# Three transposes of a four-layer kernel: from the tensor engine to 32x32 blocks on the vector engine and DMAs through DRAM

## The chip, the cores and the metric

The kernel runs on one core of a Trainium2 chip. The metric is the device time of one execution in microseconds, the lower the better. One launch computes all 32 batches; all data are float32.

## What is computed

Four residual layers follow one another on `x` of 32 batches x 256 tokens x 256 features:

```python
# L0: attention of 16 heads of 16, queries and the own key from fside
q = (seq2 + b_self) @ Wq + bq
k = concat([seq1 + b_prev, seq2 + b_self], 1) @ Wk + bk
v = concat([seq1, seq2], 1) @ Wv + bv
score_prev = q . k[:, :, :l1] * SCALE        # masked by seq_len1
score_self = (q * k[:, :, l1:]).sum(-1) * SCALE
weights = softmax(concat([score_prev, score_self], -1))
attn = weights[..., :-1] @ v[:, :, :l1] + weights[..., -1:] * v[:, :, l1:]
x = x + (attn @ Wo + bo)                                   # x1
# L1: adapter of 64, its weights chosen by a batch's id
a = x + relu(x @ W1[id] + b1[id]) @ W2[id] + b2[id]
x = x + (layernorm(a) * gamma[id] + beta[id])              # x2
# L2: linear layer chosen by a batch's id
x = x + (x @ weight[id].T + bias[id])                      # x3
# L3: pooling
scores = tanh(x @ W1 + b1) @ v
p = softmax(where(mask[type], scores[:, None, :], -1e30), -1)
x = x + (p @ x) / count(mask)
```

## The kernel before

Batches are handled in 16 pairs (`p`), two batches `i` to a pair, `b = 2 * p + i`. Each step of the work is a small function (`proj_q`, `s1`, `row_max`, ...), and tables place every call: ONCE for the set-up, FIRST, SECOND, SLOTS, NEXT_TO_LAST and LAST for the pairs 0, 1, 2 to 13, 14 and 15. A place plus 16 (`PERIOD`) for each pair is sorted, and the calls are made in that order. So the order in which each engine gets its instructions is written out by hand; the places are no times, only an order. A pair's table spans some 75 places, so four or five pairs are in the work at once: while pair `p` is in its attention, pair `p - 1` is in the adapter and pair `p - 2` in the pooling.

The attention of a batch has eight score steps, in one PSUM tile `s` of 128 x 2048 that exists once. Four of them are `s1` (L1404): the scores, which `row_max` (L1421) reads on the vector engine to find the largest of each row. The other four are `s2` (L1512): the scores again with the keys on the partitions and the maxima taken off inside the product; `exps` (L1530) reads them on the scalar engine. The maxima get into the product by DMAs on SyncE's queue: `max_own` (L1444) writes them into rows of `q`, `ones_rows` (L1433) ones into rows of `k`, `own_exp` (L1459) the own weights into `epad`. `av` multiplies by the values, `av_blocks`, `sums` and `with_own` finish the division, `att_T` (L1579) transposes by 32x32 blocks on the vector engine (the heads are laid out so that blocks are enough), and `out_proj` and `x1_out` end the first layer.

Three times after that a matrix of 256 x 256 of each batch is needed with its features (or keys) on the partitions, and each time it is transposed by the tensor engine: `x1_T`, `x2_T` and `pr_T` call `transposed` (L1157), four products with the identity into one PSUM tile; `x1T_out`, `x2T_out` and `prT_out` call `from_psum` (L1169), a copy by the scalar engine into a tile of tag `T`, which has four buffers and is shared with `attT`. The readers are `hidden` (x1), `pool_hidden` and `subject` (x2) and `pooled` (the pooling weights, which stand in `mb`).

All small products go through three PSUM tiles of tag `g`. SyncE's queue issues nearly all DMAs, in the order of the tables: `load_T` (the transposed inputs), `load_x`, `load_adapter`, `load_subject`, `load_pool`, the small ones of the attention, and `store`. `q_out` (L1325) scales the queries on the vector engine. `setup_warm` (L1047) multiplies zeros of `epad` while the first loads are under way.

Of the kernel before, what the change touches and what calls it, by code (L numbers as in the profile page):

```python
# [9 lines left out]
F32 = mybir.dt.float32  # L10
# [6 lines left out]
P = 128  # L17
# [19 lines left out]
    (("setup_warm", 2), -106.0922),  # L37
    (("setup_load", "wq"), -75.9765),
    (("setup_load", "lang"), -72.4551),
    (("setup_load", "wk"), -70.4394),  # L40
    (("setup_warm", 0), -67.4191),
    (("setup_len",), -53.0448),
    (("setup_q",), -51.9044),
    (("setup_load", "subj"), -49.8615),
    (("setup_ones",), -44.2931),
    (("setup_load", "ptype"), -33.949),
    (("setup_heads",), -33.6815),
    (("setup_warm", 1), -25.0685),
    (("setup_load", "wo"), -23.0732),
    (("setup_ks",), -19.1134),  # L50
    (("setup_load", "bo"), -16.1547),
    (("setup_k",), -14.712),
    (("setup_tw_load", 0), -14.4792),
    (("setup_mcol",), -14.1846),
    (("setup_load", "wv"), -11.1214),
    (("setup_xconst",), -6.1757),
    (("setup_tw_load", 1), -3.8083),
    (("setup_load", "pw"), -1.98),
    (("setup_vbc",), -1.4711),
    (("setup_tw_bias",), 2.7996),  # L60
    (("setup_tw", 0), 6.7491),
    (("setup_tw", 1), 7.9258),
    (("setup_tw_load", 3), 8.1898),
    (("setup_tw_load", 2), 10.5556),
    (("setup_tw", 2), 12.4314),
    (("setup_tw_load", 5), 12.6441),
    (("setup_tw", 3), 16.9719),
    (("setup_tw_load", 4), 18.7648),
    (("setup_tw", 4), 21.2344),
    (("setup_tw_load", 7), 22.4248),  # L70
    (("setup_tw", 5), 23.4443),
    (("setup_tw_load", 6), 27.4787),
    (("setup_pool",), 29.3991),
    (("setup_tw", 6), 30.1493),
    (("setup_tw", 7), 35.4648),
# [4 lines left out]
    (("load_T", "fT"), -18.0603),  # L80
    (("load_T", "xT"), -16.5929),
    (("key_mask", 0), -15.9223),
    (("mask_keys", 0), -11.5916),
    (("key_mask", 1), -9.8727),
    (("proj_q", 0), -4.2691),
    (("q_out", 0), -4.1714),
    (("mask_keys", 1), -2.9814),
    (("self_values", 0), -2.5097),
    (("vs_blocks", 0), -1.9691),
    (("proj_k", 0), -1.7792),  # L90
    (("k_out", 0, 1), -1.0305),
    (("k_out", 0, 0), -0.6291),
    (("proj_k", 1), 1.188),
    (("s1", 0, 0), 1.2724),
    (("row_max", 0, 0), 1.4111),
    (("proj_q", 1), 1.5198),
    (("k_out", 1, 0), 1.8917),
    (("k_out", 1, 1), 1.9044),
    (("q_out", 1), 2.5716),
    (("load_x",), 2.935),  # L100
    (("s1", 0, 1), 3.5652),
    (("spread_q", 0, 1), 3.7902),
    (("row_max", 0, 1), 4.0616),
    (("proj_ks", 0), 4.2676),
    (("spread_q", 1, 0), 4.4707),
    (("proj_v", 0), 4.7177),
    (("spread_q", 0, 0), 5.6696),
    (("s1", 0, 2), 5.7766),
    (("ks_out", 0), 5.7846),
    (("row_max", 0, 2), 6.3321),  # L110
    (("v_out", 0), 6.8578),
    (("proj_v", 1), 6.9271),
    (("s1", 0, 3), 7.4456),
    (("proj_ks", 1), 7.7548),
    (("row_max", 0, 3), 7.8712),
    (("v_out", 1), 7.9003),
    (("ones_rows", 0), 8.4374),
    (("s1", 1, 0), 9.1884),
    (("ks_out", 1), 9.471),
    (("row_max", 1, 0), 9.6756),  # L120
    (("own",), 9.894),
    (("own_out",), 10.0239),
    (("max_T", 0), 10.7096),
    (("spread_q", 1, 1), 10.865),
    (("s1", 1, 1), 11.0673),
    (("max_own", 0), 11.4623),
    (("row_max", 1, 1), 11.7033),
    (("s2", 0, 0), 11.7624),
    (("exps", 0, 0), 11.8784),
    (("own_exp", 0), 12.3792),  # L130
    (("s1", 1, 2), 13.3753),
    (("row_max", 1, 2), 13.7856),
    (("x_bias",), 13.9304),
    (("s2", 0, 1), 14.101),
    (("exps", 0, 1), 14.6396),
    (("s1", 1, 3), 15.0742),
    (("av", 0, 1), 15.3164),
    (("av", 0, 0), 15.4106),
    (("row_max", 1, 3), 15.4873),
    (("max_T", 1), 15.7138),  # L140
    (("s2", 0, 2), 15.8427),
    (("max_own", 1), 16.0723),
    (("exps", 0, 2), 16.1397),
    (("own_blocks", 0), 16.1874),
    (("av_blocks", 0, 0), 16.4114),
    (("s2", 0, 3), 18.02),
    (("sums", 0, 0), 18.0472),
    (("weighted", 0), 18.0754),
    (("exps", 0, 3), 18.7005),
    (("av", 0, 2), 18.9332),  # L150
    (("ones_rows", 1), 18.9624),
    (("s2", 1, 0), 20.3742),
    (("own_exp", 1), 20.473),
    (("exps", 1, 0), 21.6941),
    (("av", 0, 3), 22.9145),
    (("s2", 1, 1), 22.9621),
    (("self_values", 1), 23.0582),
    (("exps", 1, 1), 23.1594),
    (("with_own", 0, 0), 23.1667),
    (("av_blocks", 0, 1), 23.5299),  # L160
    (("vs_blocks", 1), 23.5391),
    (("sums", 0, 1), 23.8644),
    (("av", 1, 0), 23.9519),
    (("with_own", 0, 1), 24.0779),
    (("att_T", 0), 24.0955),
    (("s2", 1, 2), 24.7815),
    (("own_blocks", 1), 24.7831),
    (("out_proj", 0), 24.8791),
    (("exps", 1, 2), 25.1475),
    (("x1_out", 0), 25.405),  # L170
    (("load_adapter", 1), 25.9774),
    (("av", 1, 1), 26.02),
    (("av_blocks", 1, 0), 26.1355),
    (("s2", 1, 3), 26.4333),
    (("sums", 1, 0), 26.723),
    (("load_adapter", 0), 26.729),
    (("weighted", 1), 26.7904),
    (("exps", 1, 3), 26.8359),
    (("with_own", 1, 0), 27.1301),
    (("av", 1, 3), 27.2786),  # L180
    (("av", 1, 2), 27.3089),
    (("av_blocks", 1, 1), 28.4885),
    (("sums", 1, 1), 29.1552),
    (("x1_T", 0), 29.1691),
    (("x1T_out", 0), 29.2343),
    (("with_own", 1, 1), 29.2714),
    (("att_T", 1), 29.5256),
    (("out_proj", 1), 29.7422),
    (("x1_out", 1), 30.3052),
    (("load_subject",), 30.8005),  # L190
    (("x1_T", 1), 32.0886),
    (("x1T_out", 1), 33.0458),
    (("hidden",), 34.2518),
    (("x1_beta", 0), 34.292),
    (("x1_beta", 1), 34.8076),
    (("x1_b2", 1), 35.1038),
    (("x1_b2", 0), 35.2963),
    (("h_out",), 35.6535),
    (("adapted",), 35.9027),
    (("y_out", 0), 36.1405),  # L200
    (("y_out", 1), 36.5261),
    (("norm_stats", 0), 37.0676),
    (("norm_stats", 1), 37.0951),
    (("norm_rstd", 0), 37.6476),
    (("norm_shift", 0), 37.6554),
    (("norm_rstd", 1), 38.2154),
    (("load_pool",), 38.2983),
    (("norm", 0), 38.4629),
    (("x2_out", 0), 39.0849),
    (("x2_T", 0), 39.3257),  # L210
    (("x2T_out", 0), 39.4394),
    (("norm_shift", 1), 39.8435),
# [1714 lines left out]
```

## Time and profile before

| | us |
|---|---|
| median of 3 runs | 1056.31 |
| the three runs | 1054.40, 1056.43, 1056.31 |
| the profiled execution, its own time | 1057.54 |
| its span in the profile | 1055.7 |

| engine | busy us | share of the span | instructions |
|---|---|---|---|
| PE (TensorE) | 1035.9 | 98% | 7940 |
| DVE (VectorE) | 738.6 | 70% | 1239 |
| ACT (ScalarE) | 515.5 | 49% | 722 |
| POOL (GpSimd) | 361.9 | 34% | 489 |

The DMA engines moved 81.08 MB in 58985 packets; the packets of SyncE's queue took 25.2% of the time of 16 engines.

How to read the lines: a row of a group gives the source line, engine, operation, output <- input with their shapes and the count; then busy time and the mean duration of one in ns; then the idle time of the engine just before these instructions, and what ended it. A row of the timeline gives the start in us, the time, engine, line and operation, with the number of instructions merged into it; times of neighbouring matmuls overlap, so differences of starts are used for what one costs. The waits rows name who waited for whom: us in total, times, longest. SPq is SyncE's queue.

### The profile page before, as it was taken

Reading aid. Unit: us, or ns where it says so; the run is one execution under the profiler, and the core shown is the slowest. Engines: PE = TensorE matmul, PEld = TensorE weight load, DVE = VectorE, ACT = ScalarE, POOL = GpSimd, SP = SyncE. Lnnn points to the kernel's source line nnn. Section 1 sums busy time; section 2 is a strip of 40 time slices with the busy share of each in tenths; the row PEclk is TensorE's granted clock in tenths of the full one; section 3 lists DMA queues with packets and bytes.
Section 4 is the critical chain, followed back from the end, with each engine's and each line's share of the span. In section 5 each row is a group of like instructions: output and inputs, shape, how many; then the busy total and the mean of one; then the engine's idle time right before and its main releaser. Section 6 shows DMA issues by size and latency. Waiting matters only on the chain.

```text
span 1055.7 us, 20836 instructions
## 1 busy us (share of the span) xinstructions
PE 1035.9 (98%) x7940; PEld 599.9 (57%) x7940; DVE 738.6 (70%) x1239; ACT 515.5 (49%) x722; POOL 361.9 (34%) x489
## 2 busy tenths in 40 slices
PE   8999999999999999999999999999999999999997
PEld 5555555555555555555555556556555565555656
DVE  3766676776767677676767768677676767767675
ACT  1243454536455455554554454554545545454553
POOL 3022544233343243243324233333324323324262
PEclk9999999999999999999999999999999999999999
DMA  6131321232232211323132132312322222121231
GB/s 207 32 90 61 92 62 44 76 98 83 62 98 70 89 59 47 108 72 97 46 94 72 52 107 73 87 53 79 91 92 61 78 78 82 43 59 61 69 95 51
DMA packets 58985, 81.08 MB, mean 77 GB/s; under 512 B 7238, under 2 KB 40774, under 8 KB 58886
## 3 DMA queue, kind: packets, MB, share of 16 engines
q1 hardware_dynamic: 58358, 78.18, 25.2%
q8 instruction: 63, 1.03, 0.4%
q10 hardware_dynamic: 288, 0.79, 0.2%
q0 software_dynamic: 240, 0.79, 0.2%
q14 instruction: 36, 0.29, 0.1%
HBM read 68.45 MB, written 9.71 MB: 74 GB/s over the span
## 4 chain that ended last, share of the span: by engine, by line
PE 92%; DVE 3%; ACT 3%; DMA 1%; issue 1%; POOL 0%; SPq 0%; DVEq 0%; ACTq 0%; POOLq 0%
PE s L1521 13%; PE s L1412 13%; PE av L1543 11%; PE ksps L1313 6%; PE v_ps L1180 5%; PE qps L1313 5%; PE o_ps L1180 5%; PE p_ps L1180 5%; PE vs_ps L1180 5%; PE kps L1313 5%; PE z_ps L1180 5%; ACT e L1533 2%; PE y_ps L1654 2%; PE h_ps L1628 2%; PE t_ps L1737 2%; PE x1T_ps L1162 2%
## 5 line engine op out<-in xcount | busy, mean ns | idle before, releaser
L1533 ACT ACTIVATE e<-s 128x2048 f32<-128x2048 f32 x128 | 240.3, 1877 | 396.0 <-PE s L1521 396.0
L1425 DVE TENSOR_REDUCE nmpad<-s 128x8 f32<-128x2048 f32 x128 | 293.2, 2290 | 173.1 <-PE s L1412 172.7
L1521 PE MATMUL s<-q,k 32*128 32x256 f32 x2048 | 146.7, 400 | 3.1 <-DVE nmpad L1425 2.4
L1412 PE MATMUL s<-k,qc 32*128 32x512 f32 x1024 | 146.0, 640 | 2.5 <-ACT e L1533 1.0
L1543 PE MATMUL av<-e,vpad 128*32 128x256 f32 x2048 | 130.6, 383 | 0.0
L1521 PEld LDWEIGHTS s<-q,k 32*128 32x128 f32 x2048 | 92.5, 184 | 59.8 <-issue 25.9
L1574 POOL TENSOR_TENSOR vs<-bt,vs 128x256 f32<-128x256 f32 x64 | 46.9, 733 | 213.5 <-DVE bt L1555 213.5
L1543 PEld LDWEIGHTS av<-e,vpad 128*32 128x32 f32 x2048 | 57.6, 109 | 80.5 <-issue 39.6
L1412 PEld LDWEIGHTS s<-k,qc 32*128 32x128 f32 x1024 | 40.0, 183 | 46.5 <-ACT e L1533 29.7
L1313 PE MATMUL qps<-fT,wqs 128*128 128x512 f32 x128 | 65.1, 632 | 0.0
L1180 PE MATMUL o_ps<-wos,attT 128*128 128x256 f32 x256 | 62.7, 388 | 2.4 <-DVE pnmx L1775 1.8
L1180 PE MATMUL vs_ps<-fT,wvs 128*128 128x256 f32 x256 | 63.7, 392 | 0.0
L1180 PE MATMUL v_ps<-wvs,xT 128*128 128x256 f32 x256 | 63.5, 391 | 0.1
L1313 PE MATMUL ksps<-fT,wks 128*128 128x512 f32 x128 | 63.3, 617 | 0.0
L1313 PE MATMUL kps<-xT,wks 128*128 128x512 f32 x128 | 63.2, 617 | 0.0
L1180 PE MATMUL z_ps<-ws,x2T 128*128 128x256 f32 x256 | 62.4, 387 | 0.0
L1340 ACT ACTIVATE k<-kps,kbias,cols 128x512 f32<-128x512 f32 x64 | 46.9, 782 | 30.7 <-PE kps L1313 30.5
L1180 PE MATMUL p_ps<-x2b,prT 128*128 128x256 f32 x256 | 60.8, 381 | 0.0
L1575 POOL TENSOR_TENSOR vs<-vs,zs 128x256 f32<-128x256 f32 x64 | 39.7, 620 | 58.3 <-DVE zs L1565 56.1
L1180 PEld LDWEIGHTS vs_ps<-fT,wvs 128*128 128x128 f32 x256 | 46.1, 189 | 20.9 <-issue 12.6
L1680 POOL TENSOR_SCALAR rstd<-mv 128x2 f32<-128x2 f32 x32 | 7.9, 248 | 142.3 <-DVE mv L1673 142.3
L1180 PEld LDWEIGHTS o_ps<-wos,attT 128*128 128x128 f32 x256 | 46.8, 190 | 16.8 <-issue 5.9
(134 smaller groups left out, 1522.4 us busy)
## 6 DMA issues: line engine op xcount, KB each, us to landing
an<-in_adn SPq DMA_DIRECT2D x32, 384.0 KB
mk<-pool_d SPq DMA_DIRECT2D x32, 257.0 KB
fT<-in_fT SPq DMA_DIRECT2D x16, 512.0 KB
xs<-in_x SPq DMA_DIRECT2D x32, 256.0 KB
ws<-in_swT SPq DMA_DIRECT2D x32, 256.0 KB
out<-x2b SPq DMA_DIRECT2D x32, 256.0 KB
xT<-in_xT SPq DMA_DIRECT2D x15, 512.0 KB
wb<-in_sb SPq DMA_DIRECT2D x32, 128.0 KB
```

The costliest lines, as they stand in the source:

```text
L1162: nc.tensor.transpose(ps[:, cc, q * P : (q + 1) * P], src[:, q, cc * P : (cc + 1) * P], ident,)
L1180: nc.tensor.matmul(ps[:, q, :n], lhsT=lhsT(c, q), rhs=rhs[:, c, :], start=(c == 0), stop=(c == 1),)
L1313: nc.tensor.matmul(ps, lhsT=w[:, ci, c * P : (c + 1) * P], rhs=T[src, p][:, ci].rearrange("p b s -> p (b s)"), start=(ci == 0), stop=(ci = ...
L1340: nc.scalar.activation(joint("k", p, work, [P, 2, 2, 2, S])[:, u, c].rearrange("p b s -> p (b s)"), T["kps", p, c], AF.Identity, bias=kbia ...
L1412: nc.tensor.matmul(ps[:, j], lhsT=T["qc", p][r, c, i, q * P : (q + 1) * P], rhs=T["k", p][r, :, c, i, :], start=True, stop=True,)
L1425: nc.vector.tensor_reduce(nm_bufs[i][:, q, g : g + 8].rearrange("p (u j) -> p j u", u=2), T.pop(("s1", b, n)), AX.X, ALU.max, negate=True,)
L1521: nc.tensor.matmul(ps[:, j, k, :], lhsT=T["k", p][r, u, c, i, k * P : (k + 1) * P], rhs=T["q", p][r, u, c, i, :], start=True, stop=True,)
L1533: nc.scalar.activation(e, T.pop(("s2", b, n)), AF.Exp)
L1543: nc.tensor.matmul(ps[j * HB : (j + 1) * HB, u, :], lhsT=v_bufs[b % 3][:, k, 8 * c + 2 * j + u, :], rhs=e[:, j, k, :], start=(k == 0), sto ...
L1574: nc.gpsimd.tensor_tensor(vs, bt[:, :, :, 0:DH], vs, ALU.add)
L1575: nc.gpsimd.tensor_tensor(vs, vs, z.unsqueeze(3).to_broadcast([P, S // HB, 2, DH]), ALU.mult)
L1628: nc.tensor.matmul(ps[i * A : (i + 1) * A, :], lhsT=T["a1", b][:, c * A : (c + 1) * A], rhs=T["x1T", b][:, c, :], start=(c == 0), stop=(c ...
```

## The change

For the pairs 0 to 13 the three transposes go another way. `blocks` transposes 32x32 blocks on the vector engine (one instruction for 128 x 512), `to_dram` stores them with four DMAs, one for each group of 32 partitions, in pieces of 32 floats, so that the blocks stand in `swap_d` in the order of the transposed matrix, and `from_dram` loads it back with one DMA of 2 KB for each partition. `from_dram` waits for the stores of its matrix. The block tiles have a tag `bl` with two buffers, shared with the set-up's `sw`. NEXT_TO_LAST and LAST, the pairs 14 and 15, keep `x1_T`, `x1T_out` and the like. The transposed tiles are laid out with the row half ahead of the column half in both ways, and their readers index them so. Besides, `q_out` moves from the vector to the scalar engine; `setup_warm` reads a tile `fill` of ones, which is set first, and is called six times, not three; and every place in all six tables is new.

```diff
+    fill = work.tile([P, S], F32, tag="th", name="fill", bufs=1)
+    nc.gpsimd.memset(fill, 1.0)
...
     def setup_warm(n):
...
         for _ in range(2):
-            nc.tensor.matmul(ps, lhsT=epad[:, 0:P], rhs=epad, start=True, stop=True)
+            nc.tensor.matmul(ps, lhsT=fill[:, 0:P], rhs=fill, start=True, stop=True)
...
     def transposed(b, src, name):
-        ps = g_tile(f"{name}_ps{b}").rearrange("p (c s) -> p c s", c=2)
-        for cc in range(2):
-            for q in range(2):
-                nc.tensor.transpose(
-                    ps[:, cc, q * P : (q + 1) * P],
-                    src[:, q, cc * P : (cc + 1) * P],
-                    ident,
-                )
+        ps = g_tile(f"{name}_ps{b}").rearrange("p (q c s) -> p q c s", q=2, c=2)
+        for q in range(2):
+            for c in range(2):
+                nc.tensor.transpose(ps[:, q, c, :], src[:, q, c * P : (c + 1) * P], ident)
         T[f"{name}_ps", b] = ps
...
+    NAMES = ("x1", "x2", "pr")
+
+    def blocks(p, i, name):
+        b = 2 * p + i
+        src = T["mb" if name == "pr" else name, b]
+        bl = work.tile([P, 4, 4, HB], F32, tag="bl", name=f"{name}bl{b}", bufs=2)
+        nc.vector.transpose(
+            bl.rearrange("p k n r -> p (k n r)"),
+            src.rearrange("p q (c k e) -> p k (q c) e", c=2, e=HB),
+        )
+        T[name, "bl", b] = bl
+
+    def to_dram(p, i, name):
+        b = 2 * p + i
+        bl = T.pop((name, "bl", b)).rearrange("p k n r -> p (k n) r")
+        to = swap_d[3 * b + NAMES.index(name)].rearrange("e k n g r -> g e (k n) r")
+        for g in range(4):
+            nc.sync.dma_start(out=to[g], in_=bl[g * HB : (g + 1) * HB])
+
+    def from_dram(p, i, name):
+        b = 2 * p + i
+        t_ = work.tile([P, 2, 2, P], F32, tag="T", name=f"{name}T{b}", bufs=4)
+        nc.sync.dma_start(
+            out=t_.rearrange("p q c s -> p (q c s)"),
+            in_=swap_d[3 * b + NAMES.index(name)].rearrange("e k n g r -> k e (n g r)"),
+        )
+        T[name + "T", b] = t_
...
     def q_out(p, c):
...
-        nc.vector.tensor_scalar(qc, ps, 0.25, bcol[:, c : c + 1], ALU.mult, ALU.add)
+        nc.scalar.activation(qc, ps, AF.Identity, scale=0.25, bias=bcol[:, c : c + 1])
...
-                    rhs=T["x1T", b][:, c, :],
+                    rhs=T["x1T", b][:, :, c, :],
...
+    args.append(nc.dram_tensor("swap_d", (3 * B, 32, 4, 4, 4, 32), F32, kind="Internal").ap())
```

The steady order of the changed kernel, from one pair's first `s1` to the next pair's (pair 8 in its attention; calls on TensorE, with the transposes' steps and SyncE's calls; `x2` and so on name the matrix):

```text
s1(8,0,0)  proj_q(8,1)  max_own(7,1)  pooled(5,0)
s2(7,0,3)  av(7,0,2)  hidden(6)  store(5,0)
s1(8,0,1)  load_subject(6)  from_dram(5,1,pr)  adapted(6)  av(7,0,3)
s2(7,1,0)  proj_ks(8,0)  own_exp(7,1)
s1(8,0,2)  load_pool(6)  proj_v(8,0)  pooled(5,1)  blocks(6,0,x2)
s2(7,1,1)  self_values(7,1)  blocks(6,1,x2)  load_T(9,fT)  to_dram(6,0,x2)  proj_v(8,1)  to_dram(6,1,x2)  load_adapter(7,0)
s1(8,0,3)  proj_ks(8,1)  av(7,1,0)
s2(7,1,2)  from_dram(6,0,x2)  max_T(8,0)  from_dram(6,1,x2)  store(5,1)  own(8)  av(7,1,1)
s1(8,1,0)  out_proj(7,0)  pool_hidden(6)
s2(7,1,3)  pool_scores(6,0)  pool_scores(6,1)  ones_rows(8,0)  load_x(8)  max_own(8,0)  subject(6,1)  own_exp(8,0)
s1(8,1,1)  proj_q(9,0)  av(7,1,3)  blocks(6,0,pr)  load_T(10,xT)
s2(8,0,0)  av(7,1,2)  blocks(7,0,x1)  subject(6,0)  to_dram(7,0,x1)  from_dram(7,0,x1)
s1(8,1,2)  self_values(9,0)  to_dram(6,0,pr)  blocks(6,1,pr)  load_adapter(8,1)  av(8,0,0)
s2(8,0,1)  from_dram(6,0,pr)  proj_k(9,0)  to_dram(6,1,pr)
s1(8,1,3)  out_proj(7,1)  av(8,0,1)  blocks(7,1,x1)
s2(8,0,2)  ones_rows(8,1)  max_T(8,1)  proj_k(9,1)  to_dram(7,1,x1)  from_dram(7,1,x1)
```

## The prediction

> **What bounds the kernel now.** I read the page first, then a table of stretches one period long, then the timelines of TensorE and SyncE.
>
> ```profile
> span 1055.7 us, 20836 instructions
> PE 1035.9 (98%) x7940; PEld 599.9 (57%) x7940; DVE 738.6 (70%) x1239; ACT 515.5 (49%) x722; POOL 361.9 (34%) x489
> ...
> PE 92%; DVE 3%; ACT 3%; DMA 1%; issue 1%; POOL 0%; SPq 0%; DVEq 0%; ACTq 0%; POOLq 0%
> ```
>
> The chain that ended last is TensorE's. The stretches (busy time of PE, PEld, DVE, ACT, POOL, then clock and DMA share) say how firmly:
>
> ```profile
> 329.00:391.47 62.47, 62.47 (x489) 35.96 (x488) 44.72 (x75) 32.02 (x45) 21.81 (x29) 1.00 0.24 76
> 578.88:641.35 62.47, 62.47 (x489) 35.96 (x488) 44.72 (x75) 32.02 (x45) 21.80 (x29) 1.00 0.25 76
> ```
>
> A pair of batches takes 62.47 us, and TensorE is busy in all of them at full clock (1.00). In the middle of the kernel a microsecond taken from it is gained, if nothing else comes up. What comes up next is in its timeline, here twice in the steady part and then in the start-up, where there was too little to do:
>
> ```profile
> 645.67 0.60 PE L1162 MATMUL x2T_ps<-ident,x1b 128*128 128x128 f32 x4
> 646.20 1.14 PE L1412 MATMUL s<-k,qc 32*128 32x512 f32 x8
> ...
> 653.09 0.60 PE L1162 MATMUL x2T_ps<-ident,x1b 128*128 128x128 f32 x4
> 653.62 1.14 PE L1412 MATMUL s<-k,qc 32*128 32x512 f32 x8
> ```
>
> ```profile
> 45.42 1.98 PE L1313 MATMUL qps<-fT,wqs 128*128 128x512 f32 x4
> 47.91 1.15 PE L1521 MATMUL s<-q,k 32*128 32x256 f32 x16 [0.50 <-DVE nmpad L1425]
> ...
> 55.69 1.98 PE L1313 MATMUL kps<-xT,wks 128*128 128x512 f32 x4
> 57.75 0.71 PE L1412 MATMUL s<-k,qc 32*128 32x512 f32 x4
> ```
>
> From start to start four transposes hold TensorE for 0.53 us. And there is one PSUM tile `s`: after `s1` the next score step has to wait for `row_max`, after `s2` for `exps`. In the start-up it came 47.91 - 45.42 = 2.49 us after the end of an `s1` and 57.75 - 55.69 = 2.06 us after the end of an `s2`, whatever lay between. These are the fillings that TensorE needs in each of the 16 gaps of a period.
>
> The rows that price the rest:
>
> ```profile
> L1171 ACT COPY x2T<-x2T_ps 128x512 f32<-128x512 f32 x32 | 18.6, 586 | 14.7 <-PE x2T_ps L1162 14.7
> L1582 DVE STREAM_TRANSPOSE attT<-vs 128x512 f32<-128x512 f32 x32 | 22.6, 706 | 11.7 <-POOL vs L1575 11.7
> L1328 DVE TENSOR_SCALAR qc<-qps,bcol 128x512 f32<-128x512 f32 x32 | 23.2, 724 | 23.1 <-PE qps L1313 23.1
> L1340 ACT ACTIVATE k<-kps,kbias,cols 128x512 f32<-128x512 f32 x64 | 46.9, 782 | 30.7 <-PE kps L1313 30.5
> 628.83 0.39 SPq L1818 DMA_DIRECT2D out<-x2b  x1
> DMA  0000000000000000002599999999999997310000
> ```
>
> The last line is the DMA busy share from 628.8 to 630.8 us in slices of 0.05 us: a store of 256 KB into DRAM begins 0.9 us after its issue and is over after 1.75 us.
>
> **The change, part by part.**
>
> *Taken from TensorE.* Pairs 0 to 13 lose three transposes of two batches: 14 x 6 = 84 blocks of four, at 0.53 us: 44.5 us. Pairs 14 and 15 keep theirs.
>
> *Given back in the `s` gaps.* I laid the new table's TensorE work out in its order, with the start-to-start times of the timeline (projection 1.91, product 1.83, `av` 0.98, `hidden` 1.02, `adapted` 1.05, `own` 0.45, `max_T` 0.27 us). Before, only one gap of a steady period is short (2.00 after an `s2`, by 0.06). After, five are: 2.03 (`adapted`, `av`) after an `s1`, short by 0.46; and after an `s2` 1.91 (`proj_ks`), 1.91 (`proj_k`), 1.70 (`max_T`, `own`, `av`) and 2.00, short by 0.15, 0.15, 0.36 and 0.06. Together 1.2 us, so a period falls from 62.47 by 3.18 to 59.3 and rises to about 60.4. Ten such periods give 12 us; the same count where FIRST, SECOND and NEXT_TO_LAST take part adds 0.3, 2.9, 1.9, 1.3 and 1.4. Sum 19.8 us.
>
> *VectorE and ScalarE.* Six block transposes at 0.71 us come to VectorE, two `q_out` at 0.72 go: 44.7 + 2.8 = 47.5 of 60.4 us. ScalarE loses six copies at 0.59 and gets two `q_out` at about 0.78, as L1340. I cost both at nothing: in every stretch from one `row_max` to the next the other VectorE work leaves 1.0 us or more, but for one (6.40 us of work in 6.1 + 0.5), and the gap behind that `s1` has 3.75 us of filling. Without that cover each late `row_max` costs its lateness. I allow 0.2 us a period, 2 us. `q_out` on ScalarE has `h_out` and `spread_q` queued behind it, in a stretch with over 1 us free.
>
> *SyncE and the DMAs.* A period gets 24 `to_dram` and 6 `from_dram` issues. At the 0.33 to 0.55 us of the present issues that is about 13 us on a queue that now issues for some 20 of 62 us. `from_dram` also waits on that queue until its blocks have landed, ahead of whatever is next: behind `from_dram` of x2 stand `store`, `ones_rows`, `load_x` and `max_own`; behind that of x1 the `pr` stores or `max_own`. One matrix: four issues 1.8 us, the last begins at 1.35, lands 0.9 + 0.5 + 0.1 later; with something for the queue L = 3.1 us. `from_dram`: 0.9 + 0.7 + 0.1 = 1.7. The round trip is 4.8 us. Followed through the table: x1 of the second batch comes out of `out_proj` behind the last `s1` of its pair; from the end of that `s1`, `row_max`, `x1_out` and `blocks` are done at 3.6 us, the round trip at 8.4, and `hidden` starts at 13.0 (fillings 2.81, 2.18, 3.74 and 0.98, three score steps, and the short gap): 4.6 us over. x2 of the second batch: from the end of the third `s1`, `blocks` at 7.9 us, its stores issued from 8.1 to 9.9 behind those of the first batch and `load_T`, then `load_adapter` to 11.6, both `from_dram` by 12.4, landed by 14.5, and `pool_hidden` starts at 18.2: about 4 us over. `pr` has more than 6. The buffers of `T` (four, shared with `attT`) are free in time: each goes to the fourth next of these transposes, and its last reader stands ahead of that load in the table. So the round trips cost nothing, at this L.
>
> *The size of the pieces.* Each store goes in 2048 pieces of 128 bytes. In the trace's records of single packets, 128-byte ones (loads of the start-up) took 11 ns, 516-byte ones 28 ns, stores like loads. No row shows 128-byte stores. The Trainium skill ("DMA: Bandwidth & Descriptors", Specifications) says that under 512 bytes the engine reads, modifies and writes. By the row, 128 pieces for each of 16 engines take 1.4 us; by the rule, as an estimate with 512 bytes moved twice (2 x 27 ns), 7 us, and L is 8. I take 14 ns, near the row, and keep both ends.
>
> *Start.* Three more warm-up calls stand ahead of `setup_q`, each 1.9 us at the first ones' pace (3.78 us for two). TensorE now waits 2.5 us there for weights, and its first projections take 3.76 and 3.1 instead of 1.9 us; a warmed array may return what the calls cost. Between -3 and +5 us; I take 0. At the end the last two pairs do the same work as before in another order; that tail is held by latencies (TensorE idles for 7.7 us of its last 66), and I take 0 within 5 us either way.
>
> Sum against the profiled execution: 1057.5 - 44.5 + 19.8 + 2 = 1034.8. The median shown is 1.2 us below that execution: 1033.
>
> **The rivals.**
>
> *The round trip stops VectorE.* There are two `bl` buffers. `blocks` of `pr` of the second batch reuses that of the first, whose `to_dram` stands on SyncE behind x1's `to_dram` and the wait of x1's `from_dram`. From the end of an `s1`: x1's blocks end at 4.05, then L, 0.4 for the issue, and L again; VectorE comes to that `blocks` at 10.1 and has 1.3 us to spare before the next `row_max` delays TensorE. The stall is 2L - 6.95 us a period: nothing at 3.1, 2.1 us (all that is gained) at L = 4.5. That is reached if a 128-byte store takes 27 ns, as much as a 516-byte one, or if an issue of 512 pieces takes 0.9 us. At 8 us the stall is 9 us and the kernel ends near 1033 + 12 x 9 = 1141; at 5.5 us near 1033 + 12 x 4 = 1081. For it: two landings in series in an in-order queue. Against: the 11 ns row, and a DMA share of only 0.25.
>
> *All gaps close.* If the order overlaps better than my count, only the 44.5 us remain: 1012.
>
> *The score tile becomes the bound.* Eight times (1.07 + 2.49 + 1.08 + 2.06) is 53.6 us, under 59.3; but every stage that comes late there is paid at once. With 3 us a period lost instead of 1.2 the time is 1033 + 12 x 1.8 = 1055, no change.
>
> **How the numbers follow.** The forecast has 0.55 (its own range 1016 to 1048), closed gaps 0.08, the round trip 0.27, the score tile 0.10, of which 0.03 faster, 0.03 the same and 0.04 slower. Faster by over 0.2% (about what a measurement of this kernel can tell from no change) 0.66, the same 0.03, slower 0.31. The range of 1012 to 1092 leaves out the worst of the round trip.
>
> **What would show it.** Right: 48 transposes at the TensorE rows where there are 384; a period of about 60.4 us; TensorE idle before `s`, on `nmpad` and `e`, some 1.2 us a period; a DMA share near 0.45 (0.26, and for each period 6 x (128 x 14 + 8 x 84) ns = 15 of 60 us). Wrong: VectorE idle before `blocks` on a DMA; `hidden` or `pool_hidden` waiting for a DMA; 128-byte stores at 27 ns or more; a period over 62.5 us.

## The result and the profile after: slower by 15.7%

The changed kernel takes 1223.13 us (1213.03 to 1230.97, 6 runs), the kernel before 1056.38 (1054.4 to 1057.9): a ratio of 1.157, 95% interval 1.152 to 1.162. The forecast was 1033 us and a range to 1092.

The page of the changed kernel: span, TensorE's row, the DMA packets and the chain that ended last.

```profile
span 1221.1 us, 20972 instructions
...
PE 1075.5 (88%) x7616; PEld 584.7 (48%) x7616; DVE 780.2 (64%) x1291; ACT 494.5 (40%) x670; POOL 375.0 (31%) x490
...
DMA packets 247484, 125.15 MB, mean 102 GB/s; under 512 B 184982, under 2 KB 218518, under 8 KB 247382
...
PE 49%; DMA 19%; DVE 13%; SPq 10%; issue 4%; ACT 4%; POOL 0%; DVEq 0%; ACTq 0%; POOLq 0%
```

Before, the chain was 92% TensorE. Now half of it is something else, and 29% are the DMAs and SyncE's queue. The transposes did go (7940 to 7616 matmuls: 84 x 4 fewer, 12 more for the warm-up calls), yet TensorE is busy for longer, 1075.5 instead of 1035.9 us, and idle for 145.6 instead of 19.8. One period, with the columns as in the stretches of before:

```profile
604.58:679.20 74.62, 66.31 (x464) 35.21 (x464) 48.88 (x78) 30.43 (x41) 22.97 (x29) 0.91 0.41 106
```

74.6 us instead of 62.47, TensorE busy for 66.3 of them at a granted clock of 0.91. The waits (engine, tile and line, what ended the wait; us in all, times, longest) name what it waits for:

```profile
PE h_ps L1681 <- DMA x1T<-swap_d: 48.0, 14, 5.9
PE t_ps L1790 <- DMA x2T<-swap_d: 47.0, 18, 5.3
PE t_ps L1790 <- issue: 16.2, 7, 3.2
PE s L1574 <- DVE nmpad L1478: 8.3, 16, 1.3
PE s L1465 <- ACT e L1586: 5.3, 16, 1.0
```

`hidden` (`h_ps`) and `pool_hidden` (`t_ps`) wait for their matrix to come back from DRAM. (The row with `issue` names no releaser; it is gone, like the two above it, when nothing goes through DRAM, as an experiment below shows.) The `s` gaps, the loss that the forecast did count, are small beside that. TensorE's timeline at one such place:

```profile
640.36 0.65 PE L1681 MATMUL h_ps<-x1T,a 128*64 128x256 f32 x2
644.30 1.97 PE L1681 MATMUL h_ps<-x1T,a 128*64 128x256 f32 x6 [3.29 <-DMA x1T<-swap_d]
646.20 2.09 PE L1465 MATMUL s<-k,qc 32*128 32x512 f32 x8
648.22 1.95 PE L1707 MATMUL y_ps<-a,hT 64*128 64x256 f32 x8
650.09 1.07 PE L1596 MATMUL av<-e,vpad 128*32 128x256 f32 x16
```

The wait of 3.29 us is one half. The other is what follows: the eight products of `s` take 2.09 us, and 1.14 us in the kernel before (the row at 646.20 that the prediction shows). The six products of `h_ps` and the eight of `y_ps` are at half speed as well, and `av` at 650.09 is at full speed again. The granted clock says the same: 1.00 from 640.0 to 643.0 us, 0.51 from 644.3 to 650.0, then 1.00. So this wait is paid nearly twice: 3.29 us, and half of the 5.8 us behind it.

The Trainium skill ("TensorE: Matmul & The Clock Gate", Part 1) describes it: after a window of about 3.4 us without work TensorE goes on at half its clock until it has been busy for such a window. This trace agrees on the half and on the window: its stretches of half clock last 3.41, 6.83 or 10.24 us, but for the last, which the end of the trace cuts off. It does not agree that the window must be without work. Here the clock falls at 643.1 us, when TensorE has been idle for 2.1 us. Cut into windows of 3.41 us, the trace loses the full clock after windows with 1.76 us of idle time or more, and keeps it after those with 1.73 us or less. Over the traces of all runs the border lies between 1.6 and 2.0 us, about half of a window.

SyncE's timeline, from the stores of `pr` ahead of x1's to the loads of x2 and what stands behind them:

```profile
629.21 4.40 SPq L1216 DMA_DIRECT2D swap_d<-prbl  x4
633.71 1.51 SPq L1488 DMA_DIRECT2D k<-ones  x2
635.32 2.60 SPq L1216 DMA_DIRECT2D swap_d<-x1bl  x4
639.58 0.54 SPq L1221 DMA_DIRECT2D x1T<-swap_d  x1
...
661.37 5.33 SPq L1216 DMA_DIRECT2D swap_d<-x2bl  x8
...
669.31 1.33 SPq L1221 DMA_DIRECT2D x2T<-swap_d  x2
...
675.32 5.01 SPq L1508 DMA_DIRECT2D q<-nmT  x4
```

x1's block tile is written by VectorE at 631.2 us; its stores start at 635.3, behind those of `pr` and `ones_rows`; the load is issued at 639.6, and TensorE goes on with it at 644.3. That is 13.1 us from block tile to use, where the forecast had 4.8. For x2 both loads are issued by 670.6, and their readers start at 676.8 and 679.2, where `o_ps` ends at 673.9:

```profile
671.95 1.99 PE L1233 MATMUL o_ps<-wos,attT 128*128 128x256 f32 x8
676.77 0.66 PE L1790 MATMUL t_ps<-x2T,tw 128*64 128x256 f32 x2 [2.83 <-DMA x2T<-swap_d]
679.20 1.97 PE L1790 MATMUL t_ps<-x2T,tw 128*64 128x256 f32 x6 [1.77 <-DMA x2T<-swap_d]
```

Why a load of 256 KB is so slow is seen in the busy share of the 16 DMA engines from 640.0 to 644.5 us, in 40 slices (0.11 us each), and in the rate below it:

```profile
DMA  0000010041311322223122231222214999999632
GB/s 0 0 0 0 0 73 0 0 73 55 91 55 73 127 91 91 91 91 127 73 109 109 109 109 73 91 109 109 91 73 164 346 373 346 301 401 346 228 109 91
```

While `x1T` is loaded, the share stands at two tenths and the rate near 90 GB/s, for some 2.5 us; the load of `ws` behind it runs at nine tenths and near 350 GB/s. So only a few engines work on it. The trace's records of single packets say how many: the 128 pieces of 2 KB of this load run from 640.9 to 643.9 us, and for 2.2 of these 3.0 us exactly four are under way at a time. The Trainium skill ("DMA: Bandwidth & Descriptors", "Why a DMA increments its semaphore by 16 and not by 1") has the reason: a transfer is spread over the largest number of engines up to 16 that divides the slowest dimension of both its sides. `from_dram` reads DRAM as `k e (n g r)`, and `k` is 4, which agrees with the four packets. The forecast took its 1.7 us from a store that kept nine tenths of the engines busy.

### The profile page after: what moved, and what is told of

Same layout as the page of the kernel before. It is cut to its first block, busy times and chain, and to the rows that moved or that the text cites. A ratio compares the mean times of both kernels' runs of the same rounds, so it can differ in the third digit from the quotient of the medians.

```text
span 1221.1 us, 20972 instructions
## 1 busy us (share of the span) xinstructions
PE 1075.5 (88%) x7616; PEld 584.7 (48%) x7616; DVE 780.2 (64%) x1291; ACT 494.5 (40%) x670; POOL 375.0 (31%) x490
## 4 chain that ended last, share of the span: by engine, by line
PE 49%; DMA 19%; DVE 13%; SPq 10%; issue 4%; ACT 4%; POOL 0%; DVEq 0%; ACTq 0%; POOLq 0%
DMA x2T<-swap_d 9%; PE s L1465 8%; PE s L1574 8%; PE av L1596 6%; SPq L1216 6%; DMA x1T<-swap_d 6%; PE z_ps L1233 5%; DVE nmpad L1478 4%; ACT e L1586 3%; PE qps L1366 3%; PE vs_ps L1233 3%; DMA swap_d<-x1bl 2%; PE t_ps L1790 2%; PE ksps L1366 2%; PE h_ps L1681 2%
## 5 line engine op out<-in xcount | busy, mean ns | idle before, releaser
L1574 PE MATMUL s<-q,k 32*128 32x256 f32 x2048 | 157.6, 424 | 11.4 <-DVE nmpad L1478 8.3
L1465 PE MATMUL s<-k,qc 32*128 32x512 f32 x1024 | 155.9, 680 | 8.8 <-ACT e L1586 5.3
L1596 PE MATMUL av<-e,vpad 128*32 128x256 f32 x2048 | 136.6, 386 | 0.0
L1574 PEld LDWEIGHTS s<-q,k 32*128 32x128 f32 x2048 | 98.5, 196 | 75.1 <-issue 30.8
L1790 PE MATMUL t_ps<-x2T,tw 128*64 128x256 f32 x128 | 39.5, 562 | 65.3 <-DMA x2T<-swap_d 47.0
L1828 DVE CUSTOM_DVE_ANT_0 mb<-sc_ps,mk 128x256 f32<-128x256 f32 x64 | 24.1, 415 | 110.0 <-PE sc_ps L1818 110.0
L1561 POOL TENSOR_TENSOR vs<-vs,eown 128x256 f32<-128x256 f32 x64 | 43.2, 695 | 127.6 <-DVE eown L1526 117.2
L1681 PE MATMUL h_ps<-x1T,a 128*64 128x256 f32 x128 | 34.0, 492 | 48.0 <-DMA x1T<-swap_d 48.0
L1233 PE MATMUL z_ps<-ws,x2T 128*128 128x256 f32 x256 | 67.8, 411 | 5.3 <-DMA x2T<-swap_d 5.3
L1805 ACT ACTIVATE th<-t_ps,tw 64x256 f32<-64x256 f32 x32 | 15.0, 469 | 133.1 <-PE t_ps L1790 132.7
```

The source lines that it names most:

```text
L1233: nc.tensor.matmul(ps[:, q, :n], lhsT=lhsT(c, q), rhs=rhs[:, c, :], start=(c == 0), stop=(c == 1),)
L1465: nc.tensor.matmul(ps[:, j], lhsT=T["qc", p][r, c, i, q * P : (q + 1) * P], rhs=T["k", p][r, :, c, i, :], start=True, stop=True,)
L1574: nc.tensor.matmul(ps[:, j, k, :], lhsT=T["k", p][r, u, c, i, k * P : (k + 1) * P], rhs=T["q", p][r, u, c, i, :], start=True, stop=True,)
L1596: nc.tensor.matmul(ps[j * HB : (j + 1) * HB, u, :], lhsT=v_bufs[b % 3][:, k, 8 * c + 2 * j + u, :], rhs=e[:, j, k, :], start=(k == 0), sto ...
L1681: nc.tensor.matmul(ps[i * A : (i + 1) * A, :], lhsT=T["a1", b][:, c * A : (c + 1) * A], rhs=T["x1T", b][:, :, c, :], start=(c == 0), stop= ...
L1790: nc.tensor.matmul(ps[i * A : (i + 1) * A, :], lhsT=T["tw", b][:, c * A : (c + 1) * A], rhs=T["x2T", b][:, :, c, :], start=(c == 0), stop= ...
```

## The experiments

**The load by 16 engines.** The DRAM side of `from_dram` split by hand, so that each of four loads has 32 partitions as its slowest dimension.

```diff
-        nc.sync.dma_start(
-            out=t_.rearrange("p q c s -> p (q c s)"),
-            in_=swap_d[...].rearrange("e k n g r -> k e (n g r)"),
-        )
+        to = t_.rearrange("p q c s -> p (q c s)")
+        fr = swap_d[...].rearrange("e k n g r -> k e (n g r)")
+        for k in range(4):
+            nc.sync.dma_start(out=to[k * HB : (k + 1) * HB], in_=fr[k])
```

> from_dram is issued as four loads of 32 partitions each, in place of one of 128; nothing else differs. Theory A: the one load moves slowly because only about 4 of the 16 DMA engines carry it (its side in DRAM begins with a dimension of 4), so it lands 4.7 us after its issue and not 1.7, TensorE idles about 3.3 us before hidden and 4.6 us before pool_hidden, and then runs at half clock. Then the four loads land in about 3 us in all, the two waits fall below 3 us, the half clock goes, and the time falls to 1070 to 1120. Theory B: SyncE's queue is what is late (issues and waits for landings in order). Then 18 more issues a period make it later: 1221 to 1260. Theory C: the 128-byte pieces fill the DMA engines. Then nothing moves: 1210 to 1230.

Measured: 1110.98 us, ratio 1.052 (1.050 to 1.054): 112 of the 167 us are gone by this alone. Its waits, and a load with its reader:

```profile
PE h_ps L1681 <- DMA x1T<-swap_d: 24.7, 11, 4.2
PE t_ps L1790 <- DMA x2T<-swap_d: 16.5, 21, 4.0
```

```profile
595.14 1.71 SPq L1224 DMA_DIRECT2D x1T<-swap_d  x4
...
598.48 1.05 PE L1681 MATMUL h_ps<-x1T,a 128*64 128x256 f32 x6 [1.79 <-DMA x1T<-swap_d]
```

The reader runs 3.3 us after the start of the issue, not 4.7, though the four issues take 1.2 us longer than the one. The 128 pieces are the same, but five to nine are now under way at a time for most of it. Less than half of the waiting is left, and much of it is too short to bring half clock: `h_ps` behind a wait of 1.79 us runs at full speed (1.05 us for six products, 1.97 above). The granted clock is 0.986 in the mean, 0.932 before this edit.

**The wait filled with other work.** Twelve products of 256 columns, whose result is overwritten, ahead of `hidden` and of `pool_hidden`; then six.

```diff
+        for _ in range(12 if p < NP - 2 else 0):
+            nc.tensor.matmul(ps, lhsT=ident, rhs=wqs[:, 0, :], start=True, stop=True)
```

> As the changed kernel, with 12 products of no use ahead of the first product of hidden and of pool_hidden (pairs 0 to 13), 2.9 us each time, in the waits for the loads. If half of the loss is the clock that falls after an idle wait (a mean granted clock of 0.932, so some 83 us), the clock returns to about 1.00 and the time falls by 60 to 84 us to 1135 to 1165. If the slow stretches after a wait are waits of another kind (reads of late operands), it stays at 1221 or rises by up to 70 us.

> As the changed kernel, with 6 products of no use ahead of the first product of hidden and of pool_hidden (pairs 0 to 13). A float32 product is two instructions of 0.24 us in these traces, so 6 are 2.9 us, less than the waits they stand in (the 12 of the run before were 5.8 us, more than the waits). If the fallen clock costs some 80 us by itself: TensorE's busy time without these products falls from 1075 to about 1000 and the time to 1125 to 1165. If the clock matters little: 1200 or more.

Measured: 1199.99 us with twelve (ratio 1.136, 1.134 to 1.139) and 1198.9 with six (1.132, 1.128 to 1.137), both slower than the first case of their expectations and a little faster than the second. The page with twelve, and the rows of its fillings:

```profile
PE 1160.2 (97%) x8288; PEld 688.7 (57%) x8288; DVE 780.3 (65%) x1291; ACT 494.0 (41%) x670; POOL 373.8 (31%) x490
...
L1679 PE MATMUL h_ps<-wqs,ident 128*128 128x256 f32 x336 | 76.2, 383 | 0.0
L1790 PE MATMUL t_ps<-wqs,ident 128*128 128x256 f32 x336 | 76.0, 383 | 0.0
```

The fillings held TensorE for 152.2 us in all, twice what I had counted, since such a product takes 152.2 / 336 = 0.45 us in fp32, as two instructions; without them TensorE is busy for 1160.2 - 152.2 = 1008.0 us, against 1075.5 in the changed kernel. That much, 67.5 us, is the half clock: work that is the same, done at full speed (a granted clock of 0.997). Idle time fell by 107.6 us to 38. With six, 27.6 us of the half clock are left (1114.6 - 79.0 = 1035.6 us), because 2.8 us of filling don't cover all waits (32.0 us are left for x2 and 19.3 for x1), and what the shorter fillings save is lost to that. So both parts of the loss are real and of this size, but filling buys back only 23 to 24 of the 167 us: it takes the time that the wait took.

**No way through DRAM at all.** The blocks stay, stores and loads go, and the products read the matrices as they lie, which leaves out the transposition.

```diff
-        for g in range(4):
-            nc.sync.dma_start(out=to[g], in_=bl[g * HB : (g + 1) * HB])
...
-        nc.sync.dma_start(
...
+        src = T["mb" if name == "pr" else name, b]
+        T[name + "T", b] = src.rearrange("p q (c s) -> p q c s", c=2)
```

> The changed kernel's order with blocks kept on VectorE, but no stores and loads through DRAM: hidden, pool_hidden, subject and pooled of pairs 0 to 13 read the matrices untransposed, so that part of the computation is changed. It shows what the order gives when the transposes cost TensorE nothing and the round trip takes no time. If the forecast's sum was right but for the round trip: 1028 to 1045. If the order itself holds the loss (short gaps at the score tile, waits for PSUM tiles): over 1060.

Measured: 1034.38 us, ratio 0.979 (0.977 to 0.980). Its page:

```profile
span 1032.6 us, 20274 instructions
...
PE 1007.4 (98%) x7616; PEld 560.2 (54%) x7616; DVE 778.0 (75%) x1291; ACT 492.8 (48%) x670; POOL 374.8 (36%) x490
```

This is close to the forecast's sum (1033 us), which is a sum for everything but the round trip. It is the baseline for the rest. Against it the changed kernel's TensorE is busy for 1075.5 - 1007.4 = 68.1 us more and idle for 145.6 - 25.2 = 120.4 us more; together they are the 188.5 us between the spans. The 68 us agree with the 67.5 of the fillings.

**The way through DRAM, with nobody waiting for it.** Stores and loads issued at their places as in the change, the readers again on the untransposed matrices; once with one load a matrix and once with four.

```diff
-        T[name + "T", b] = t_
+        src = T["mb" if name == "pr" else name, b]
+        T[name + "T", b] = src.rearrange("p q (c s) -> p q c s", c=2)
```

> The changed kernel with every block operation, every store and every load through DRAM issued at its place, but the weight products, the pooling products and the pooled values read the matrices as they lie in SBUF, not transposed: this leaves out the transposition, so that no product waits for a load from DRAM. If the 167 us are the latency of the round trip alone (the readers' waits and the half clock behind them), this runs as the kernel without the round trip did, 1030 to 1045 us. If a good part of them is what the issues do to SyncE's queue (a later `q<-nmT`, later loads of x, ws and the adapter) and what the transfers do to other loads, some of the loss stays: 1060 to 1110 us. I hold the first for likelier (0.6), since the readers' waits add up to nearly the idle time.

> The same with each load from DRAM as four loads of 32 partitions; again the products read the matrices untransposed, so that the transposition is left out. Against the kernel with four loads (1111 us) it takes away the readers' waits alone. If what is left there, 77 us over the kernel without the round trip, is the readers' remaining wait (24.7 and 16.5 us in the trace) with its half clock, this gives 1034 to 1050 us. If it is SyncE's queue (18 loads more a pair, at some 0.5 us each), 1070 to 1105 us; then it also stands above the kernel with single loads that nobody waits for, by what the 18 issues cost.

Measured: 1057.39 us with one load (ratio 1.001, 0.999 to 1.003) and 1060.52 with four (1.004, 1.003 to 1.005). This divides the loss:

| | one load a matrix | four loads |
|---|---|---|
| nothing through DRAM | 1034.4 | 1034.4 |
| issues and transfers alone | +23.0 | +26.1 |
| readers wait for them | +165.7 | +50.5 |
| the time | 1223.1 | 1111.0 |

The traffic alone takes back all that the transposes had freed. The waits of the version with one load show one way by which it does so: `s2` waits for the maxima that `max_own` sends, which it did not with nothing going through DRAM. These are 6 of the 15 us by which TensorE's idle time grew; the rest is in many small waits that I did not follow.

```profile
PE s L1575 <- DMA q<-nmT: 6.0, 2, 4.7
```

SyncE holds `max_own` behind a transfer. In the trace of the change it waits there 21 times until a load of `x2T` has landed, which `max_own` doesn't read:

```profile
SPq L1508 <- DMA x2T<-swap_d: 36.1, 21, 3.3
```

SyncE's DMAs signal eight semaphores in turn in this trace, and each waits for the one eight before it. Both times lie between the two cases that I expected: the readers' wait is the larger part, but the first case was too low by 10 to 12 us.

**The new order by itself.** All three transposes back on TensorE at the place of `from_dram`, with a copy by ScalarE; then the same with only the pooling weights through DRAM, by four loads.

```diff
+        if name in ON_PE:
+            transposed(b, T["mb" if name == "pr" else name, b], name + "T")
+            from_psum(b, name + "T")
+            return
```

> The changed kernel's order of all steps, its q_out on ScalarE and its warm-up, but all three transposes by TensorE and the copy by ScalarE at the place of from_dram; no blocks, no stores and loads through DRAM. Theory A: the order itself is not what costs; the transposes fill some of its short gaps, and it takes 1055 to 1080. Theory B' (the new places are what loses, by short gaps at the score tile): 1120 or more.

> The changed kernel's order, x1 and x2 transposed by TensorE at the place of from_dram, the pooling weights alone by blocks and DRAM, loaded with four DMAs. The pooling weights have over 6 us to spare. Theory A: their round trip is hidden, 28 of 84 blocks of transposes (14.8 us) are gone from TensorE, less some gaps: 1040 to 1065. Theory B or C (any such round trip hurts through SyncE's queue or the DMA engines): over 1090.

Measured: 1090.17 us (ratio 1.032, 1.030 to 1.034) and 1071.01 (1.014, 1.012 to 1.016), each between its two cases. The new order is one for a kernel without these transposes: with them a period takes 65.2 us, by the starts of `t_ps` in the timelines, instead of 62.47, and TensorE waits for 13.1 us in all with `own` behind the copy of x2 and for 10.0 with `s` behind `e`. Given that order, 14 pairs of pooling weights through DRAM gain 19 us: this matrix has the time for its round trip (TensorE's list shows no wait for it). For x1 and x2 the waits above show that they do not.

**The stores on another queue.** As the version with four loads, the stores issued from ScalarE (`nc.scalar.dma_start`).

```diff
-            nc.sync.dma_start(out=to[g], in_=bl[g * HB : (g + 1) * HB])
+            nc.scalar.dma_start(out=to[g], in_=bl[g * HB : (g + 1) * HB])
```

> The changed kernel with four loads a matrix (1111 us), and the stores to DRAM issued from ScalarE's queue instead of SyncE's. If SyncE's queue makes the round trip long (the stores stand behind other issues and hold them up), the loads land some 2 us earlier and the queue's other loads run on time: 1065 to 1095 us. If the latency of stores and loads themselves is what is left, 1100 to 1120 us. ScalarE pays some 2.5 us a matrix, 15 us a pair, for the issues; it is busy for half of the span, so if its exponents come late by that, `s` waits for `e` and it is slower: 1120 to 1180 us.

Measured: 1102.42 us, ratio 1.044 (1.042 to 1.046), a little better than with SyncE (1.052). By the time this is my second case; by the waits it is a trade:

```profile
PE ksps L1366 <- DVE vs L1544: 31.3, 10, 3.1
PE s L1465 <- ACT e L1586: 13.1, 17, 3.8
...
PE h_ps L1681 <- DMA x1T<-swap_d: 5.7, 5, 1.7
```

The wait for x1 falls from 24.7 to 5.7 us and that for x2 (16.5 us) leaves the list: what had been left of them came from the stores on SyncE's queue. But ScalarE is held for 6 to 10 us by the eight stores of an x2, and TensorE now waits for `e` and, on `ksps`, for a PSUM tile that VectorE frees late. How the second follows from the first was not traced.

**The order of before, with some matrices through DRAM.** Pairs 2 to 13 alone, in before's order: the pooling weights, then x1 too. In the first two runs I put the loads of `pr` behind `load_subject`; in the next two ahead of it, with `blocks` and `to_dram` earlier; the lines show the third run against the first. (The first with x1 also has the second batch's `pr` later than the first without.)

```diff
-    (("blocks", 0, "pr"), 46.3061),   (("to_dram", 0, "pr"), 46.4),   (("from_dram", 0, "pr"), 47.2),
-    (("blocks", 1, "pr"), 46.3062),   (("to_dram", 1, "pr"), 46.5),   (("from_dram", 1, "pr"), 47.5),
+    (("blocks", 0, "pr"), 45.54),     (("to_dram", 0, "pr"), 45.55),  (("from_dram", 0, "pr"), 46.29),
+    (("blocks", 1, "pr"), 46.3061),   (("to_dram", 1, "pr"), 46.31),  (("from_dram", 1, "pr"), 47.3),
```

> The kernel before with its own order; only the pooling weights of pairs 2 to 13 go by blocks and DRAM, blocks right after x1_out of the next pair (10 us ahead of their reader at the least), one load of 128 partitions each. Theory A (the path pays where its latency of about 9 us is covered): 24 blocks of transposes at 0.53 us leave TensorE, two of its gaps at the score tile become short by 0.15 and 0.26 us a period, so about 8 us less: 1044 to 1053. Theory B (SyncE's queue and its order make any such path a loss): 1058 or more.

> As h1_pr, and x1 of pairs 2 to 13 by blocks and DRAM as well (x2 stays on TensorE): blocks of its first batch ahead of q_out, of its second right after x1_out, both over 14 us ahead of hidden. Theory A: 48 blocks of transposes gone, four gaps short by 0.15 to 0.26 us: about 15 us less: 1036 to 1050. Theory B: 1060 or more.

> The kernel before with only the pooling weights (pairs 2 to 13) through VectorE's blocks and DRAM, in the order of before; the blocks stand right behind `pool_mask`'s exponents, the stores behind them, and the loads from DRAM ahead of the loads of the next adapter, where the last try had them behind `load_subject`. It takes 12 pairs x 16 transposes x 0.13 us = 25 us less a small gap a pair off TensorE. If the loss of the last try (1153 us) was the place in SyncE's queue, `p_ps` finds its matrix there and the time is 1032 to 1053 us. If the round trip itself is too long for the stretch between `pr` and `p_ps` (some 7 us), `p_ps` waits 2 to 5 us a pair and runs at half clock behind it: 1080 to 1150 us.

> The same with x1 as well, its blocks right behind `x1_out`, its loads from DRAM ahead of the adapter's loads. It takes another 25 us off TensorE. If both round trips are covered in this order, 1015 to 1045 us, faster than with the pooling weights alone; if x1's round trip (some 9 us from the issue of the stores to the landing of the load) is longer than the stretch to `hidden` allows, `h_ps` waits and it is slower than with the pooling weights alone, by 12 pairs x 2 to 4 us, 1065 to 1100 us.

Measured: 1153.14 us (ratio 1.091, 1.090 to 1.093) and 1162.48 (1.100, 1.099 to 1.102) with the late loads; 1109.22 (1.048, 1.045 to 1.050) and 1177.64 (1.116, 1.114 to 1.118) with the early ones. None came near the better of its cases, and the last is beyond both. With late loads `p_ps` waits (the first row, from the first run). With early ones it no longer does (1.1 us), and yet the kernel loses 53 us, and `v_ps` waits instead (the second row, from the third run):

```profile
PE p_ps L1211 <- DMA prT<-swap_d: 68.9, 12, 13.0
...
PE v_ps L1211 <- DVE x1c L1695: 29.6, 8, 4.1
```

In the third run SyncE's queue issues the load of x^T behind both loads of `prT`; then, on GpSimd, VectorE and TensorE:

```profile
653.61 0.42 SPq L1269 DMA_DIRECT2D xT<-in_xT  x1
...
660.26 0.19 POOL L1278 COPY first<-xT 128x2 f32<-128x2 f32 x1 [20.52 <-DMA xT<-in_xT]
660.41 1.22 POOL L1539 TENSOR_TENSOR vs<-vs,eown 128x256 f32<-128x256 f32 x2
661.58 2.50 POOL L1650 TENSOR_TENSOR x1b<-x,an 128x512 f32<-128x512 f32 x2
664.03 2.49 POOL L1635 TENSOR_TENSOR x1c<-x,an 128x512 f32<-128x512 f32 x2
666.55 0.69 DVE L1695 TENSOR_TENSOR x1c<-y_ps,x1c 128x512 f32<-128x512 f32 x1 [4.20 <-POOL x1c L1635]
...
667.30 1.99 PE L1211 MATMUL v_ps<-wvs,xT 128*128 128x256 f32 x8 [3.25 <-DVE x1c L1695]
```

Read it from below: `v_ps` waits behind `x1c` on VectorE, that for `x1_b2` on GpSimd, and GpSimd had sat for 20.5 us at a copy of x^T (8.9 at this copy in the kernel before), whose load stood behind the round trip on SyncE. The reader of the transposed matrix is hardly late, and time is lost all the same, three engines further on. This wait is 29.6 of the 45.5 us by which TensorE's idle time grew (65.3 us, 19.8 before); the rest was not followed. With x1 as well, `s` also waits for `ones_rows` (`k<-ones`), 32.9 us in 9 waits, on the same queue.

**The same with x^T ahead of the loads.** Pooling weights only, the stores on ScalarE, four loads a matrix behind x^T.

```diff
-    (("from_dram", 0, "pr"), 46.29),
-    (("from_dram", 1, "pr"), 47.3),
+    (("from_dram", 0, "pr"), 47.42),
+    (("from_dram", 1, "pr"), 47.44),
...
-            nc.sync.dma_start(out=to[g], in_=bl[g * HB : (g + 1) * HB])
+            nc.scalar.dma_start(out=to[g], in_=bl[g * HB : (g + 1) * HB])
```

> The order of before with the pooling weights alone through DRAM (pairs 2 to 13), stores on ScalarE's queue, loads (four a matrix) on SyncE's queue right behind the load of x^T. If the last try's 1109 us came from the late load of x^T (the first copy of it on GpSimd, then `x1c`, then `v_ps` waiting 4 us), this gives 1035 to 1060 us. If the pooling weights land too late for `p_ps` now, or `e` comes late by the 5 us of issues on ScalarE, it stays at 1070 to 1110 us.

Measured: 1156.74 us, ratio 1.094 (1.093 to 1.096), beyond both cases. The load of x^T is in front now, and the wait has moved to ScalarE:

```profile
662.49 4.88 ACTq L1194 DMA_DIRECT2D swap_d<-prbl  x4
667.42 1.88 ACT L1564 ACTIVATE e<-s 128x2048 f32<-128x2048 f32 x1 [6.32 <-DMA swap_d<-prbl]
...
669.35 2.09 PE L1443 MATMUL s<-k,qc 32*128 32x512 f32 x8 [8.23 <-ACT e L1564]
...
PE s L1443 <- ACT e L1564: 87.1, 14, 8.4
```

Four stores hold ScalarE for 4.9 us, the exponents stand behind them, and TensorE stands for 8.2 us and goes on at half clock. The last row has the sum of these waits. The wait of `v_ps` behind `x1c` is gone from the list, and GpSimd waits for x^T as long as in the kernel before (127.9 us in all, 126.1 before), which speaks for the reading of the run with early loads. It does not settle it, as the wait for `e` may cover what is left.

**No DMA: VectorE does the whole transpose.** Sixteen transposes a matrix, each from one group of 32 partitions to another; pooling weights, then x1 too, in the order of before.

```diff
+        for k in range(4):
+            for g in range(4):
+                nc.vector.transpose(to[k * HB : (k + 1) * HB, g], src[g * HB : (g + 1) * HB, k])
```

> The order of before with the pooling weights of pairs 2 to 13 transposed by VectorE alone: 16 transposes a matrix, each of 32 partitions by 128 elements from one group of 32 partitions to another, so that nothing goes through DRAM. TensorE loses 12 pairs x 16 x 0.13 = 25 us. VectorE gains 32 instructions a pair; from the rows of 0.69 us for 512 elements and 0.45 for 256, about 0.33 us each (an estimate), 10.6 us a pair, by which it goes from 70% to some 85% busy. If the loss of the earlier tries was the way through DRAM and VectorE's work fits beside TensorE's, 1028 to 1050 us. If VectorE's stretch of 5.3 us a matrix makes `row_max` or the sums late, `s` waits for VectorE: 1056 to 1090 us.

> The same with x1 too: another 25 us off TensorE and another 10.6 us a pair on VectorE, which then has all of the pair's 62 us to work (44 + 21 = 65 us at the estimated 0.33 us an instruction). If the instructions are as long as that, VectorE is the bound: 1080 to 1150 us. If they are nearer 0.2 us, 1020 to 1050 us.

Measured: 1130.51 us (ratio 1.071, 1.070 to 1.073) and 1245.3 (1.179, 1.177 to 1.181), both beyond the worse of their cases. An instruction of 32 x 128 takes 0.30 us, near the estimate, but they come in one piece:

```profile
647.75 5.04 DVE L1181 STREAM_TRANSPOSE prT<-mb 32x128 f32<-32x128 f32 x16
```

```profile
PE s L1533 <- DVE nmpad L1437: 50.1, 19, 4.8
PE nm_ps L1453 <- DVE nmpad L1437: 10.4, 10, 1.5
```

`row_max` stands behind the 5 us, and TensorE waits for it, up to 4.8 us, and goes on at half clock. With the pooling weights alone VectorE is only 76% busy: it is not its time that is short, but the time between one `row_max` and the next. No version that still transposes beat the kernel before.

## Why the prediction was wrong, by its own steps

*"So the round trips cost nothing, at this L."* This step failed, in three of its terms, which the traces measure at the two places shown.

- *"`from_dram`: 0.9 + 0.7 + 0.1 = 1.7."* It took 4.7 us for x1. For two x2 in a row it was 7.5 and about 9 us from a load's issue to its reader; from the end of both issues (670.6 us) to the later reader it was 8.6 us, where the prediction had 2.1, and that alone is more than x2's slack of about 4. The row it came from was a store that kept nine tenths of the engines busy; this load had four of 16. Replacing it by four loads won back 112 us.
- *"four issues 1.8 us"*, *"L = 3.1 us"*. The four issues took 2.6 us at the least and 4.5 at the most, with a median of 0.63 us for one store of 64 KB where I had put 0.45. From x1's first store to the issue of its load it was 4.3 us (635.32 to 639.58), and 4.2 at the least over all 28 of x1.
- The stores were taken to be issued when the blocks are done. For x1 they started 4.1 us later, behind those of `pr` and `ones_rows`. I had added up SyncE's issues (13 on 20 of 62 us) and found room, but not followed the queue at this place. With these three, 4.1 + 1.2 + 3.0 = 8.3 us against a slack of 4.6, x1 is late by 3.7; the trace has 3.3.

*A late step "costs its lateness".* So I priced stalls, in the sum and in the rivals. Half clock adds some 68 us to about 120 us of waiting in this kernel. The prediction had no term for it. Nor had it one for the issues and transfers themselves, 23 us in the run in which no reader waits for them.

*Rival "the round trip stops VectorE".* Its sign was right, and so was the queue in order: x1's stores at 635.3 stand behind those of `pr`. Its place was not: VectorE waited for a store once, for 0.7 us, and L, 4.4 us in the median over x1, was just under the 4.5 us at which it was to decide. The 1.8 us a period that its formula gives for 4.4 did not come; TensorE's own readers were hit first. Its upper numbers (1081 to 1141) were too low as well.

*"44.5 us" off TensorE and "19.8" given back.* The sum held: 1034.4 us without the round trip, 1033 forecast. Not each term did, so that it came so near is in part luck. A steady period there takes 61.27 us, by the starts of `t_ps`, so the gaps cost 2.0 us and not 1.2 + 0.2. Against that, the first `s1` came at 20.4 us instead of 24.6 (21.0 in the changed kernel), where I had put the start at nothing, between -3 and +5. What is left was not followed.

*"I take 14 ns" for a piece of 128 bytes.* Right: 13 ns in the mean over the trace's 172,000 packets of that size. The rule of the Trainium skill ("DMA: Bandwidth & Descriptors", Specifications), from which I had estimated 7 us a matrix, doesn't show in this trace. The DMA time was right too: 0.41 of 74.6 us is 31 us, and 0.26 of 62.47 us with the 15 us of the new transfers is 31. The share of 0.45 that the prediction gave does not follow from these terms: 31 of 60.4 us is 0.51.

*VectorE, ScalarE and the score tile.* `s` waits for `nmpad` and `e` for 13.6 us in all; `q_out` on ScalarE shows in no wait of TensorE.

## What to carry to other kernels

Price a transfer by its access pattern, not by its bytes: look at the slowest dimension of both sides, and take a row of the trace only from a transfer that is spread alike. Follow a new DMA through its queue at the very place, with what is issued before it and what is queued behind it; a queue with room on average can hold a load for 4 us, and the late one may be a transfer that has nothing to do with the change. On TensorE waits of some 3 us were paid nearly twice at the place shown, and one and a half times over the whole kernel (188.5 us lost for 120.4 us of waiting), so slack must cover the slowest case and not the mean. Idle time of up to 1.6 us in a window of 3.4 us had no such second price here.

## What was not expected of the hardware

- Half clock needed no idle window of 3.4 us: it came after 2.1 us of idle time at 643.1 us and after 2.8 us at 677.2 us. In the changed kernel's trace it followed windows of 3.41 us with 1.76 us of idle time or more, and ended after a window with at most 0.14 us.
- A store of 64 KB in 512 pieces of 128 bytes held SyncE for 0.55 to 2.5 us; four of them in a row held SyncE for 2.6 to 4.5 us, and ScalarE for 4.9 us in the lines above.
- An fp32 product of 256 columns with 128 rows took 0.45 to 0.47 us as a filling, in two instructions.
- Stores in pieces of 128 bytes took 13 ns a piece in the mean, with no sign of a second pass.
